# Two small products on a column of each value tile, ahead of the weighted sums of a local attention block

## The chip, the cores and the metric

The kernel runs on one core of one Trainium2 chip. The time is the device time in microseconds (us) of one execution; a kernel is run several times and the median is given. The profile is of one further execution, and its span runs from the first to the last instruction of the program.

## The reference

The input is 16 sequences of 256 rows with 128 features. After a layer norm, two branches are computed from it: a Mamba-like branch (projection, short convolution, a selective scan with 16 states) and a stack of six layers of local attention and feed-forward. The result is `x + s * silu(g)`. The part that matters here is the attention of the second branch, in float32:

```
q, k, v = split(x @ Wqkv)            # 16 heads of 64
q, k = normalized, scaled, rotated
windows of 32 queries; each sees its own 32 keys and the 32 before
sim  = q @ k.T * 8, masked
attn = softmax(sim)
out  = attn @ v                      # per head and window: 32x64 times 64x64
x    = out @ Wo + x
```

## The kernel before, in words

The attention is worked off in 192 blocks: six layers, 16 sequences, two blocks of 128 rows each. All of it is one program with an order written out by hand: the table `order` (lines 759 to 807) lists the steps of one turn of the main loop, and each step takes the block `n + ahead`. So one turn works on up to six blocks at different stages, and every engine executes its instructions in the order in which this table issues them. The semaphores between engines and DMA queues are put in by the framework from what each instruction reads and writes.

The steps around the change are these, for block `n`:

- `values` (472) multiplies the rows by the value weights (L427) into PSUM banks 4 and 5. `hand_out` (475) copies the result with ScalarE (L480) into the tile `vt`, in which every head has 64 value columns and a 65th that is one. Then SyncE issues DMAs that bring `vt` into `v2`: for each of two halves `r` (64 partitions, every second head) and each of four windows `j`, the 64 rows of keys that window `j` sees. An even block of a sequence takes 8 such DMAs (L492, L494), an odd one 10 (L491, L492, L494). `v2` exists once for even and once for odd blocks. `hand_out` of block `n + 1` stands just before `attend` of block `n`.
- `score` (575) lays the mask into PSUM (L587) and adds the products of queries and keys (L601): for eight column groups `c`, four windows `j` and two halves `r` one product with 64 rows and 32 columns of the array. A product in float32 is two weight loads and two matmuls in the records of the profile, so a block has 128 of each.
- `greatest` (L614) and `subtract` (L624) on VectorE, `soften` (L633) on ScalarE, then `turn_weights` (L552) transposes the weights and `turned_weights` copies them from PSUM into `aT` with ScalarE (L556).
- `attend` (644) makes the weighted sums (L657), again 64 products on tiles of 64 rows and 32 columns: tile (64 r, 32 j) of the array, weights `aT[rr, c, jj]`, moving `v2[rr, j, 65 columns of c]`. It takes `c = 7` first, into a bank of its own for each half (banks 7 and 6, `pav7`), then `c = 0` to `6` into banks 2 and 3 (`pav`), from which `subtract` of the following block has read the scores before. The 65th column of each sum is the softmax denominator.
- `divide_last` (665) takes the reciprocal of the denominators of `c = 7` on VectorE (L673) and scales on ScalarE (L674); `divide` (676) does the others on VectorE (L680, L681). `turn_out` transposes the result, `turned_out` copies it (L556), `close` (701) multiplies by `Wo` (L708).

Within one turn, TensorE's work ahead of `attend` is `project` of the keys of block `n + 4` and `values` of block `n + 1` (four L427 records each); the ScalarE step `square` (L438) of the queries, which reads banks 6 and 7, lies before it too. Behind it comes `turn` of the queries of block `n + 2` (L552). A scan step of the other branch and a part of a feed-forward (L326 to L375) are laid between these steps in every turn.

Of the kernel before, what the change touches and what calls it, by code (L numbers as in the profile page):

```python
# [18 lines left out]
H, DH, W = 16, 64, 32  # L19
# [11 lines left out]
def tile_kernel(ctx: ExitStack, tc: tile.TileContext, a, out):  # L31
    nc = tc.nc
# [14 lines left out]
    def pair(name):  # L47
        i = int(where[name])
        return psum[:, i : i + 2, :].rearrange("p b x -> p (b x)")

    def bank(name):
        return psum[:, int(where[name]), :]
# [591 lines left out]
    def attend(n):  # L644

        b = blocks[n]
        aT, v2 = b["aT"], v2s[b["blk"]]

        b["pav"] = pair("av").rearrange("p (r x) -> p r x", r=2)[:, :, 0 : 7 * VW]
        b["pav"] = b["pav"].rearrange("p r (c d) -> p r c d", c=7)  # L650
        b["pav7"] = [bank("e"), bank("l")]
        for c in (7, 0, 1, 2, 3, 4, 5, 6):
            for j in range(4):
                jj = slice(j * W, (j + 1) * W)
                for r in range(2):
                    rr = slice(r * 64, (r + 1) * 64)
                    nc.tensor.matmul(  # L657
                        b["pav7"][r][jj, 0:VW] if c == 7 else b["pav"][jj, r, c, :],
                        aT[rr, c, jj],
                        v2[rr, j, c * VW : (c + 1) * VW],  # L660
                        start=True,
                        stop=True,
                    )
# [87 lines left out]
    def feed():  # L751
# [35 lines left out]
        (rotate2, 4, 1),  # L787
        (add, 4, 1),
        (attend, 0),
        (divide_last, 0),  # L790
        (state, None, drive),
# [142 lines left out]
```

## Time and profile before

| | us |
|---|---|
| median of three runs | 3447.9 |
| lowest and highest | 3443.46, 3448.29 |
| the profiled execution, its own time | 3446.38 |
| its span | 3444.6 |

The granted TensorE clock of that execution has a mean of 0.988. The page of the profile gives the busy time of each engine (PE is TensorE's matmuls, PEld its weight loads, DVE is VectorE, ACT ScalarE, POOL GpSimd, SP SyncE, which only issues DMAs), the chain of work that ended last, and the costliest groups of instructions: line, engine, operation, the names of what is written and read, shapes, count, then busy time, the mean of one in ns, and the idle time of its engine just before it with what ended it. "issue" stands for waiting for nothing that the profile shows.

The rows of the steps around the change that are not taken up below:

```profile
L427 PE MATMUL psum<-wqkv,xT 128*128 128x512 f32 x2304 | 1070.3, 600 | 18.6 <-DVE cv L227 7.2
...
L438 ACT ACTIVATE sq<-psum 128x1024 f32<-128x1024 f32 x384 | 395.0, 1029 | 51.4 <-DVE t L459 51.0
...
L657 PEld LDWEIGHTS psum<-v,aT 64*32 64x32 f32 x24576 | 294.0, 105 | 200.9 <-issue 121.9
...
L480 ACT COPY vt<-psum 128x1024 f32<-128x1024 f32 x192 | 196.2, 1022 | 189.6 <-PE psum L427 189.6
...
v<-vt SPq DMA_DIRECT2D x1152, 130.0 KB, 2.4
```

The last of them is a row of the DMA issues: the transfers of L494, 1152 of them, of 130 KB each, take 2.4 us in the median from issue to landing. Busy time is a union, so records that overlap are counted once; the mean of one is its whole latency, which for a matmul on a small tile is much longer than the distance to the next one.

### The profile page before, as it was taken

The page shows a single profiled execution, that of the slowest core. Times are in us where ns is not written, and L with a number is a line of the kernel's source. Part 1 is how long each engine was busy: PE and PEld are TensorE (multiplying, and loading weights), DVE is VectorE, ACT ScalarE, POOL GpSimd, SP SyncE. Part 2 cuts the span into 40 slices and gives each one's busy share as a digit, 9 for nine tenths or more (in the row PEclk, how much of TensorE's full clock was granted, in tenths as well). Part 3 has the DMA queues.
Part 4 walks back from the last instruction along what each step waited for, and adds up shares of the span by engine and source line. Part 5 has one row for each costly group of instructions (what it writes and reads, how often), then busy time and mean ns, then how long its engine had stood idle before and what let it go on. Part 6 is the DMA issues. An engine that isn't in the chain of part 4 may idle for free.

```text
span 3444.6 us, 139812 instructions
## 1 busy us (share of the span) xinstructions
PE 3238.9 (94%) x62080; PEld 2163.4 (63%) x62080; DVE 2810.2 (82%) x3705; ACT 2123.3 (62%) x2725; POOL 2598.0 (75%) x2358
## 2 busy tenths in 40 slices
PE   6999999999999999999999999999999999999986
PEld 3666666666666666666666666666666666666663
DVE  6898879887898789878987889788879987777663
ACT  4666657655666566656665666576666665666554
POOL 6688868986898589968996789688878996565550
PEclk9999999999999999999999999999999999999998
DMA  3433334433333334333333333334333432222222
GB/s 87 104 98 105 84 84 104 104 81 83 97 97 90 91 94 97 91 85 88 107 92 91 88 96 92 89 99 98 91 81 93 105 94 70 69 64 70 63 64 57
DMA packets 190680, 304.49 MB, mean 88 GB/s; under 512 B 32702, under 2 KB 56572, under 8 KB 190076
## 3 DMA queue, kind: packets, MB, share of 16 engines
q1 hardware_dynamic: 189788, 295.22, 33.9%
q8 instruction: 488, 8.00, 1.0%
q14 instruction: 116, 0.95, 0.1%
q10 hardware_dynamic: 288, 0.33, 0.0%
HBM read 94.81 MB, written 8.91 MB: 30 GB/s over the span
## 4 chain that ended last, share of the span: by engine, by line
PE 73%; DVE 12%; ACT 6%; POOL 5%; issue 4%; DMA 0%; SPq 0%; DVEq 0%; ACTq 0%; POOLq 0%
PE psum L427 23%; PE psum L552 14%; PE psum L708 9%; PE psum L657 7%; PE psum L349 7%; PE psum L601 6%; PE psum L372 3%; ACT oT L556 3%; DVE t L459 2%; DVE o L681 2%; PE psum L587 2%; DVE hs L288 1%; DVE t L448 1%; POOL t L470 1%; DVE cv L227 1%
## 5 line engine op out<-in xcount | busy, mean ns | idle before, releaser
L470 POOL TENSOR_TENSOR t<-t,t 128x1024 f32<-128x1024 f32 x384 | 957.1, 2502 | 355.0 <-DVE t L459 184.4
L427 PE MATMUL psum<-wqkv,xT 128*128 128x512 f32 x2304 | 1070.3, 600 | 18.6 <-DVE cv L227 7.2
L542 POOL TENSOR_TENSOR t<-t,y 128x1024 f32<-128x1024 f32 x384 | 723.1, 1905 | 7.5
L427 PEld LDWEIGHTS psum<-wqkv,xT 128*128 128x128 f32 x2304 | 417.4, 192 | 406.0 <-issue 304.5
L448 DVE TENSOR_TENSOR t<-psum,tab 128x1024 f32<-128x1024 f32 x384 | 467.9, 1219 | 143.9 <-PE psum L427 131.1
L556 ACT COPY aT<-psum 128x1024 f32<-128x1024 f32 x192 | 194.2, 1012 | 589.6 <-PE psum L552 589.6
L459 DVE TENSOR_TENSOR t<-psum,tab 128x1024 f32<-128x1024 f32 x384 | 465.9, 1213 | 0.0
L504 DVE TENSOR_REDUCE ss<-sq 128x16 f32<-128x1024 f32 x384 | 456.4, 1198 | 1.3
L552 PE MATMUL psum<-ident,t 128*128 128x128 f32 x3072 | 412.7, 277 | 20.8 <-POOL t L542 8.9
L438 ACT ACTIVATE sq<-psum 128x1024 f32<-128x1024 f32 x384 | 395.0, 1029 | 51.4 <-DVE t L459 51.0
L657 PEld LDWEIGHTS psum<-v,aT 64*32 64x32 f32 x24576 | 294.0, 105 | 200.9 <-issue 121.9
L708 PE MATMUL psum<-oT,wo 128*128 128x256 f32 x1536 | 357.5, 386 | 24.2 <-ACT oT L556 24.2
L657 PE MATMUL psum<-v,aT 64*32 64x65 f32 x24576 | 332.8, 227 | 47.0 <-issue 24.6
L552 PEld LDWEIGHTS psum<-ident,t 128*128 128x128 f32 x3072 | 340.4, 142 | 40.3 <-POOL t L542 11.7
L708 PEld LDWEIGHTS psum<-oT,wo 128*128 128x128 f32 x1536 | 283.8, 190 | 81.4 <-ACT oT L556 46.5
L480 ACT COPY vt<-psum 128x1024 f32<-128x1024 f32 x192 | 196.2, 1022 | 189.6 <-PE psum L427 189.6
L601 PEld LDWEIGHTS psum<-kT,qT 64*32 64x32 f32 x24576 | 282.8, 105 | 11.2 <-issue 0.8
L601 PE MATMUL psum<-kT,qT 64*32 64x64 f32 x24576 | 286.2, 226 | 0.0
L288 DVE TENSOR_TENSOR_SCAN hs<-dA,bc 128x512 f32<-128x512 f32 x128 | 277.3, 2166 | 0.0
L556 ACT COPY oT<-psum 128x1024 f32<-128x1024 f32 x192 | 194.8, 1014 | 124.9 <-PE psum L552 123.0
L349 PE MATMUL psum<-xn,w 128*128 128x512 f32 (+1 forms) x576 | 260.2, 601 | 6.0 <-ACT o L674 4.8
L624 DVE TENSOR_TENSOR at<-psum,top 128x1024 f32<-128x1024 f32 x192 | 235.1, 1225 | 25.3
(102 smaller groups left out, 4583.0 us busy)
## 6 DMA issues: line engine op xcount, KB each, us to landing
v<-vt SPq DMA_DIRECT2D x1152, 130.0 KB, 2.4
bc<-rows SPq DMA_DIRECT2D x128, 512.0 KB, 5.1
v<-vt SPq DMA_DIRECT2D x576, 65.0 KB, 2.5
wqkv<-in_Wqkv SPq DMA_DIRECT2D x18, 512.0 KB, 4.0
wo<-in_Wo SPq DMA_DIRECT2D x6, 512.0 KB, 4.0
first<-in_x SPq DMA_DIRECT2D x8, 256.0 KB, 5.0
xn<-xT SPq DMA_DIRECT2D x16, 128.0 KB, 2.4
pad<-xn SPq DMA_DIRECT2D x8, 256.0 KB
```

The costliest lines, as they stand in the source:

```text
L349: nc.tensor.matmul(ph[0:n, i * G : (i + 1) * G], w1[:, i * DI + c0 : i * DI + c0 + n], xn, start=True, stop=True,)
L427: nc.tensor.matmul(pq[:, cc], xb, wq[:, cc], start=True, stop=True)
L448: nc.vector.tensor_tensor(t1.rearrange("p (h d) -> p h d", h=H), b["pq", i].rearrange("p (h d) -> p h d", h=H), table(n, i, 0).unsqueeze(1 ...
L459: nc.vector.tensor_tensor(t2.rearrange("p (h f d) -> p h f d", h=H, f=2), b["pq", i].rearrange("p (h f d) -> p h f d", h=H, f=2)[:, :, ::- ...
L470: nc.gpsimd.tensor_tensor(b["qk", i], b["qk", i], b["t2", i], ALU.add)
L504: nc.vector.tensor_reduce(b["ss"][:, j * H : (j + 1) * H], b["sq", i].rearrange("p (h d) -> p h d", h=H), AX.X, ALU.add,)
L542: nc.gpsimd.tensor_tensor(t3, t3, b["inv"][:, j * H : (j + 1) * H].unsqueeze(2).to_broadcast([128, H, DH]), ALU.mult,)
L552: nc.tensor.transpose(pt[:, cc], of[:, cc], ident)
L556: nc.scalar.copy(to, pt.rearrange("p (c t) -> p c t", c=NP))
L601: nc.tensor.matmul(sc4[jj, r, c, :], qT[rr, c, jj], kT[rr, c, k0 : k0 + 64], start=False, stop=True, skip_group_check=True,)
L657: nc.tensor.matmul(b["pav7"][r][jj, 0:VW] if c == 7 else b["pav"][jj, r, c, :], aT[rr, c, jj], v2[rr, j, c * VW : (c + 1) * VW], start=Tru ...
L708: nc.tensor.matmul(b["pw"][:, 0:L], wo[:, c, :], b["oT"][:, c, :], start=(c == 0), stop=(c == NP - 1), skip_group_check=True,)
```

## The change

Ahead of the 64 weighted sums of a block, two more products are issued, one for each half `r`. The weights are those of the sum for `c = 7`, window 0; the moving operand is column 0 of the four slices of `v2` of that half, 64 rows and 4 columns with a stride of one slice. They write the corner of 32 partitions and 4 columns of the two banks `pav7`, which the sums of `c = 7`, `j = 0` write afterwards with `start=True`. Nothing reads what they compute. The rest of the kernel is as before.

```diff
@@ -649,6 +649,12 @@
         b["pav"] = pair("av").rearrange("p (r x) -> p r x", r=2)[:, :, 0 : 7 * VW]
         b["pav"] = b["pav"].rearrange("p r (c d) -> p r c d", c=7)
         b["pav7"] = [bank("e"), bank("l")]
+
+        for r in range(2):
+            rr = slice(r * 64, (r + 1) * 64)
+            nc.tensor.matmul(
+                b["pav7"][r][0:W, 0:4], aT[rr, 7, 0:W], v2[rr, :, 0], start=True, stop=True
+            )
         for c in (7, 0, 1, 2, 3, 4, 5, 6):
             for j in range(4):
                 jj = slice(j * W, (j + 1) * W)
```

## The prediction

> **What bounds the kernel now.** First the page: its busy line, then the chain of work that ended last, then the rows of the two groups of small products.
>
> ```profile
> PE 3238.9 (94%) x62080; PEld 2163.4 (63%) x62080; DVE 2810.2 (82%) x3705; ACT 2123.3 (62%) x2725; POOL 2598.0 (75%) x2358
> ...
> PE 73%; DVE 12%; ACT 6%; POOL 5%; issue 4%; DMA 0%; SPq 0%; DVEq 0%; ACTq 0%; POOLq 0%
> PE psum L427 23%; PE psum L552 14%; PE psum L708 9%; PE psum L657 7%; PE psum L349 7%; PE psum L601 6%; PE psum L372 3%; ACT oT L556 3%; DVE t L459 2%; DVE o L681 2%; PE psum L587 2%; DVE hs L288 1%; DVE t L448 1%; POOL t L470 1%; DVE cv L227 1%
> ...
> L657 PE MATMUL psum<-v,aT 64*32 64x65 f32 x24576 | 332.8, 227 | 47.0 <-issue 24.6 <-DVE at L624 14.4 <-ACT sq L438 6.6
> ...
> L601 PE MATMUL psum<-kT,qT 64*32 64x64 f32 x24576 | 286.2, 226 | 0.0
> ```
>
> TensorE sets the end: 94% busy, 73% of the chain, and L657, the weighted sums that the change precedes, has 7% of it. A DMA is nowhere in the chain. The odd thing is in the last two rows. Both groups have 24576 records (two for each float32 product, 128 a block in 192 blocks) on the same 64*32 tiles; L657 streams 65 columns instead of 64 (1.6% more), yet is busy 332.8 against 286.2 us, 16% more: 46.6 us, or 243 ns a block. That is beside its idle time.
>
> Where do these 243 ns lie? I took one block from the timeline:
>
> ```profile
> 1013.55 0.19 PEld L427 LDWEIGHTS psum<-wqkv,xT 128*128 128x128 f32 x1 [0.24 <-ACT aT L556]
> ...
> 1015.79 1.70 PE L657 MATMUL psum<-v,aT 64*32 64x65 f32 x128
> ...
> 1017.60 0.25 DVE L680 RECIPROCAL den<-psum 128x14 f32<-128x14 f32 x1 [0.54 <-PE psum L657]
> ```
>
> and asked in 10 ns windows how many L657 matmuls are in flight (the x), then the same of this block's L601:
>
> ```profile
> 1016.00:1016.01 0.01, 0.01 (x28) 1.00 0.00 0
> 1016.10:1016.11 0.01, 0.01 (x23) 1.00 0.00 0
> 1016.25:1016.26 0.01, 0.01 (x6) 1.00 0.00 0
> 1016.40:1016.41 0.01, 0.01 (x11) 1.00 0.00 0
> 1016.55:1016.56 0.01, 0.01 (x16) 1.00 0.00 0
> 1016.70:1016.71 0.01, 0.01 (x27) 1.00 0.00 0
> ...
> 1010.20:1010.21 0.01, 0.01 (x19) 1.00 0.00 0
> 1010.30:1010.31 0.01, 0.01 (x21) 1.00 0.00 0
> 1010.45:1010.46 0.01, 0.01 (x27) 1.00 0.00 0
> ```
>
> The clock is full (1.00). The sums start well (x28), fall to 6 for a third of their time, and recover; the scores never fall below 19. The single records say the same: over all blocks (medians), matmul 32 starts 268 ns after the first, matmul 48 at 673 ns, matmul 127 at 1479 ns: 8.4 ns a record, then 405 ns for 16 records (25 ns each), then 10.2 ns. In the slow stretch two records start every 42.5 ns. The trace's semaphore record has what beats with it: TensorE's own semaphore is raised at 1016.104, .146, .189, .231, .274, .316, .359 and .401, eight times, 42.5 ns apart; matmuls start at 1016.142, .151, .193, .229, .236, .272, .278. Eight is the number of products for c = 7. In the program that this kernel builds to, each of these eight carries one wait (ScalarE, or one DMA semaphore) and each adds one to TensorE's semaphore; of the 56 behind them only the first waits (VectorE, L624), and only what others await adds, near the end (1 to 5 times). An addition stands on a product somebody awaits, or on one whose successor waits, because it can't be put off past a wait. Of the eight only the last two, j = 3, are awaited (L673). So the reading: the waits themselves cost nothing, since all are satisfied; **the additions that they force cost TensorE a slow stretch**.
>
> **The change, part by part.**
>
> *It removes* the waits of the eight products. Both small products read column 0 of all four v2 slices of their half and column group 7 of aT, thus everything the eight wait for. L657's own c = 0 to 6 show that a second reader of a slice gets no wait. What is left in this stretch: additions on the first small product (the second one waits) and on the two awaited ones: three instead of eight. Price of one: at the later pace of 10.2 ns the 16 slow records would take 163 ns instead of 405; 242 ns over eight is 30 ns. Five less: 151 ns a block. Bounds: the full spacing, 5 x 42.5 = 212 ns; from below nothing, if the stretch has another cause. The Trainium skill (TensorE: Matmul & The Clock Gate, "The cost: per-tile semaphore tail") says that increments of concurrent tiles serialize at some 26.3 ns each, and that one on the last is enough: 5 x 26.3 = 132 ns by the rule. The row decides: 151.
>
> *It adds* two products, in float32 four weight loads and four matmul records of 4 columns, on tiles (0,0) and (64,0). As stream: 4 x 10.2 = 41 ns. A rule speaks against this: TensorEngine Tiling, "Instruction Overhead", has a product with one column take as long as one with 60. By the rule the two tiles go through 18 full passes instead of 16; at 1479/16 = 92 ns a pass that is 185 ns, more than the saving. The trace sits between: eight records start in 56 ns in the queued part at the start, so a tile can turn a 65-column pass in 56 ns (two: 112 ns), while the later pace is 8 x 10.2 = 82 ns a pass; a tile that lags by 112 ns can catch up 26 ns a pass over 14 passes. I take the stream's 41 ns and keep 0 and 185 as ends. They write the corner [0:32, 0:4] of the banks that c = 7 then overwrites on the same engine; nobody reads it.
>
> *It moves* waits to the front: for an even block one ScalarE and eight DMA semaphores now stand before the first weighted sum, for an odd one ten DMAs. An instruction holds one wait, the others become semaphore instructions on TensorE's queue, 51 ns each by L657's rows: I count 4 (even) or 5 (odd) where there are 1 or 2 now, so 3 x 51 = 153 ns more. What hides it: in the timeline TensorE's sequencer is held by aT until 1013.47 and by the square (which ends 1014.40), and after that it runs ahead of the four L427 records until 1015.79, 1.4 us. Cover gone, it is 153 ns a block, 23 us in all. Queued behind are 128 sums, whose end L680 awaits. The DMAs: v2 of a block is issued one turn before its use (issues at 1000.00 to 1005.88 for the sums at 1015.79), landing takes 2.4 us in the median, 6.3 at most: long there, so demanding j = 3 first costs nothing. No DMA, no ScalarE, VectorE, POOL or SP instruction is added or moved.
>
> *The sum:* 151 - 41 = 110 ns a block. How much counts: L657's 7.4% of the chain (the chain's own answer) is 255 us, in pieces of 1.63 to 1.72 us, thus 153 of 192 blocks; and L680 waits for L657 153 times (113.0 us). 153 x 0.110 = 16.8 us. Before a matmul of L657 TensorE stood idle for "issue" 21 times, 24.6 us, each time with a 16 KB instruction transfer begun 2.2 to 2.9 us earlier; such a block (11%) gives its gain back to the fetch: 15 us. What is late next is the old chain, shifted: L680, L681, the turn of o. From the profiled span of 3444.6 us (3446.4 with what lies around it) this makes 3431; from the median of 3447.9, which I use, **3433 us**.
>
> The instruction stream is an unknown of its own. Each block gets 8 records and about 3 semaphore instructions more, so the places where fetches fall shift against the blocks. "issue" idles on TensorE come to some 40 us in all; their positions drift through the blocks and come back about every 430 us. With another drift I expect the same sum, give or take 10 us.
>
> **Rivals.**
> 1. *As forecast*, chance 0.62: 3433, between 3424 (212 - 30 ns) and 3441.
> 2. *The products take back the gain*, 0.19: the two first tiles lag by two full passes and the rest waits for them. 151 - 185 = -34 ns, or at 56 ns a pass +39: between +5 and -6 us, so 3448 or thereabouts. For it: the rule, and the 82 ns a pass. Against: the slack of 26 ns a pass.
> 3. *Slower: the additions aren't the cause*, 0.13. Then the stretch is TensorE's queue run dry (it begins after 33 loads and 33 matmuls, where what was queued during L427 would end), it stays, and the change is pure added work: 41 to 185 ns x 153 blocks, +6 to +28 us: 3465 in the middle. It decides if less than 41 of the 242 ns are the additions'. Against it: the 42.5 ns beat, and that L601, queued as long behind L587, has no such stretch.
> 4. *The change doesn't do what it says*, 0.06: the waits stay on the eight, for instance as a semaphore is awaited anew for each slice; 153 x 41 ns is 6 us, 3454. Against: c = 0 to 6.
>
> **How the numbers follow.** What this measurement can tell from no change is about 0.2%, 7 us (the three runs spread by 4.9). Faster: most of the first case and a bit of the second with luck in the fetches, 0.67. Same: the rest of the first, most of the second, half of the fourth, 0.20. Slower: the third and the other half, 0.13. The range reaches from 3405, the full 212 ns with every block on the chain, no cost of the products (-36 us) and good fetches, to 3451, where the second case ends; the third's middle lies outside. The first case's own range is 3424 to 3441.
>
> **What would show it.** In the changed profile L657 (both small products get a line of their own) should be busy some 1.6 us a block instead of 1.73, about 310 us in all; the windows should have no stretch of 6 in flight, but two or three short dips; semaphore instructions of TensorE rise to about 860 on the new line; L680's wait shrinks by about 0.1 us a time. If L657 keeps 330 us, the third case holds; if the dip is gone but the end of the sums isn't earlier, the second. A DMA named as the releaser of the small products would make the whole argument wrong.

## The result, and the profile after

The changed kernel takes 3460.51 us in the median of 16 runs (3448.23 to 3470.26), the kernel before 3447.03 in 16 runs on the same chips (3437.98 to 3453.92). The ratio is 1.0040, with a 95% interval of 1.0029 to 1.0052: slower by 0.4%, where 0.4% faster was forecast, and outside the range. The profiled execution has a span of 3461.4 us.

The page after, in the same parts as before: busy time by engine, the chain that ended last, and the row of the weighted sums, which are now on L663.

```profile
PE 3241.1 (94%) x62848; PEld 2157.8 (62%) x62848; DVE 2807.5 (81%) x3705; ACT 2118.5 (61%) x2725; POOL 2593.1 (75%) x2358
...
PE 71%; DVE 12%; POOL 6%; ACT 5%; issue 4%; DMA 0%; SPq 0%; DVEq 0%; POOLq 0%; ACTq 0%
...
L663 PE MATMUL psum<-v,aT 64*32 64x65 f32 x24576 | 317.5, 226 | 57.1 <-issue 45.2
```

The sums have become shorter, 317.5 us of busy time after 332.8 (about 310 was forecast). But the idle time before them that ended for no visible reason ("issue") has grown from 24.6 to 45.2 us; in a second profile of each kernel it is 27.6 and 36.6 us. VectorE's reciprocal (L680, now L686), which waits for the last sums, stood waiting for 119.7 us in all where it was 113.0; forecast was 0.1 us less each time. The two small products are a line of their own; this is what the view of one source line says of it (count, then shortest, median and longest duration in ns):

```profile
L655 PEldq EVENT_SEMAPHORE  x863: 51/51/51, 71.2 to 3408.6; - x173
...
L655 PE MATMUL psum<-v,aT x768: 164/169/213, 73.4 to 3408.8; 64*32 64x4 f32 x192
```

So 863 semaphore instructions stand where 286 did, as counted in the prediction (some 860). Next, the matmuls of L663 in flight in 10 ns windows, in the block whose windows were shown of before; the offsets from its first sum are about the same.

```profile
1022.06:1022.07 0.01, 0.01 (x23) 1.00 0.00 0
1022.21:1022.22 0.01, 0.01 (x13) 1.00 0.00 0
1022.36:1022.37 0.01, 0.01 (x19) 1.00 0.00 0
```

The stretch with 6 in flight is gone; what is left is a short dip to 13. By the single records (medians over the blocks), the last sum starts 1362 ns after the first instead of 1479, and the first one 549 ns after the last value product instead of 523. From that product to the last sum it is 1911 ns where it was 2002: **the change saves 91 ns a block, and the kernel is still slower.**

Where the time went can be seen in one block. TensorE's timeline of the changed kernel, and after it that of the kernel before in a block that lies in about the same place of the instruction stream:

```profile
1506.83 1.53 PE L663 MATMUL psum<-v,aT 64*32 64x65 f32 x121
1509.38 0.27 PE L663 MATMUL psum<-v,aT 64*32 64x65 f32 x2 [1.02 <-issue]
```

```profile
2161.84 1.70 PE L657 MATMUL psum<-v,aT 64*32 64x65 f32 x128
```

In the changed kernel TensorE stops for 1.02 us in front of the last two records of the sums, with no semaphore to wait for. The trace of DMA packets tells what it waits for. TensorE's instructions come in transfers of 16384 bytes, 256 instructions each (488 of them for the 124,979 instructions of the kernel before). These are the packets around the two blocks, of the changed kernel from 1506.7 to 1506.8 us (a digit is 2.5 ns), and of the kernel before from 2160.8 to 2161.0 us (5 ns):

```profile
DMA  0000000000000000000000090000000000000000
q8 instruction: 1, 0.02, 82.1%
```

```profile
DMA  0000000090000000000000000000000000000000
q8 instruction: 1, 0.02, 30.1%
```

In the changed kernel the transfer begins at 1506.76, 0.04 us *before* the first sum (1506.80), and the sums go on 2.62 us after that; in every such stall of the two profiles it is 2.2 to 3.0 us. In the block of the kernel before, the transfer begins at 2160.84, 1.00 us before the first sum (2161.84), and nothing stops. A block of the changed kernel consumes its 256 instructions of sums in 1.4 us. So the start of the transfer decides, and the change moved it by about one microsecond.

That these gaps are waits for instructions can be seen by counting: over the 17 kept traces TensorE has 661 gaps for "issue", and behind all but 2 of them the next instruction has the same place in the stream, number 193 or 194 of a group of 256.

### The profile page after: what moved, and what is told of

Read it like the earlier page. It is cut to its first block, busy times and chain, and to the rows that moved or that the text cites. A ratio compares the mean times of both kernels' runs of the same rounds, so it can differ in the third digit from the quotient of the medians.

```text
span 3461.4 us, 141925 instructions
## 1 busy us (share of the span) xinstructions
PE 3241.1 (94%) x62848; PEld 2157.8 (62%) x62848; DVE 2807.5 (81%) x3705; ACT 2118.5 (61%) x2725; POOL 2593.1 (75%) x2358
## 4 chain that ended last, share of the span: by engine, by line
PE 71%; DVE 12%; POOL 6%; ACT 5%; issue 4%; DMA 0%; SPq 0%; DVEq 0%; POOLq 0%; ACTq 0%
PE psum L427 22%; PE psum L552 13%; PE psum L714 9%; PE psum L349 7%; PE psum L663 7%; PE psum L601 6%; PE psum L372 3%; ACT oT L556 3%; DVE t L459 2%; POOL t L542 2%; DVE hs L288 2%; DVE o L687 2%; POOL t L470 1%; PE psum L587 1%; DVE t L448 1%
## 5 line engine op out<-in xcount | busy, mean ns | idle before, releaser
L438 ACT ACTIVATE sq<-psum 128x1024 f32<-128x1024 f32 x384 | 395.0, 1029 | 51.2 <-DVE t L459 51.2
L714 PE MATMUL psum<-oT,wo 128*128 128x256 f32 x1536 | 357.5, 386 | 24.4 <-ACT oT L556 24.4
L663 PE MATMUL psum<-v,aT 64*32 64x65 f32 x24576 | 317.5, 226 | 57.1 <-issue 45.2
L663 PEld LDWEIGHTS psum<-v,aT 64*32 64x32 f32 x24576 | 275.1, 105 | 67.8 <-issue 52.4
```

The lines of the kernel that those rows point to most:

```text
L663: nc.tensor.matmul(b["pav7"][r][jj, 0:VW] if c == 7 else b["pav"][jj, r, c, :], aT[rr, c, jj], v2[rr, j, c * VW : (c + 1) * VW], start=Tru ...
L714: nc.tensor.matmul(b["pw"][:, 0:L], wo[:, c, :], b["oT"][:, c, :], start=(c == 0), stop=(c == NP - 1), skip_group_check=True,)
```

## The experiments

The quantities below come from each kernel's trace. *Issue idle*: gaps over 150 ns between TensorE's matmuls that ended for "issue"; *short* are those under 1.5 us each, *long* the others. *Transfer start*: the median start of an instruction transfer against the first sum, for even and odd blocks of a sequence; negative is earlier. It is taken in the blocks where the end of a transfer's 256 instructions falls into about the last 50 of the sums, so that it can stall them, from transfers begun in the 2 us around the first sum (from 1.7 before to 0.3 after). A median is over 3 to 19 transfers, single ones lie more than 1 us off it, and other limits move some medians by 0.1 to 0.2 us. A figure after a stroke is a second profile.

| kernel | ratio to before | issue idle, us | of it short, us | transfer start even, odd (us) | first to last sum, ns |
|---|---|---|---|---|---|
| before | 1 | 38.2 / 45.0 | 22.1 / 21.6 | -1.14, -0.22 | 1479 |
| the change | 1.0040 | 60.2 / 50.2 | 41.2 / 33.7 | -0.05, -0.07 | 1362 |
| odd blocks alone | 1.0056 | 50.3 / 49.0 | 22.0 / 26.6 | -1.14, -0.11 | both kinds |
| even blocks alone | 1.0042 | 53.0 | 29.4 | -0.07, -0.24 | both kinds |
| products behind c = 7 | 1.0050 | 53.3 / 42.0 | 23.6 / 20.1 | -1.19, -0.21 | 1513 |
| one such product | 1.0040 | 43.4 | 24.4 | -1.17, -0.13 | 1495 |
| one product over 128 rows | 0.9976 | 24.0 | 10.8 | -0.95, -0.82 | 1324 |
| a transfer cut in two | 1.0034 | 45.2 / 51.3 | 28.4 / 28.5 | -0.25, -0.14 | 1481 |
| stream shifted by 128 | 0.9993 | 36.1 | 15.9 | -1.16, -0.42 | 1479 |
| bf16 product ahead | 0.9917 | 15.8 | 8.8 | -1.42, -0.82 | 1324 |
| the same and the change | 0.9951 | 16.2 | 10.6 | -1.25, -1.13 | 1362 |
| bf16 and products behind c = 7 | 0.9945 | 18.8 | 10.1 | -1.26, -0.58 | 1358 |

The second profiles of the first two rows missed what was expected of them. The kernel before was to show 38 us of issue idle again, within 5, and showed 45.0; the change was to show 60 us within 8, of them 41 us within 5 in short ones, and showed 50.2 and 33.7. So such a sum moves by 7 to 10 us from one execution to the next. The places are steadier: of the 21 blocks of the kernel before whose sums stalled for issue, 17 stalled in both profiles, and of 39 of the change, 30.

The row of before holds the first lead: its odd blocks are as late as the change's. In the program, an odd block has one more DMA behind the window 0 of each half than an even one, so that its *second* sum needs two waits; in this program a weight load holds one of them, and a semaphore instruction with the other stands between the first and the second sum. Even blocks have none there. The change puts two between its two small products in every block. **Theory A:** such an instruction behind the first product of the block keeps TensorE's sequencer from running ahead, and with it the request for the next instructions. **Theory B:** it is the number of added instructions, or the faster sums, that brings more blocks into stalls.

### One half of the change at a time

```diff
-        for r in range(2):
+        for r in range(2 if b["blk"] == 1 else 0):
```

> The two small products in odd blocks alone. A stall is the time by which the start of the last weighted sum of a block lies later than usual, without those in which VectorE is awaited at record 16: 31.0 us in 27 blocks before, 58.5 us in 44 blocks after. Theory A (a semaphore instruction between the first two products of a block keeps TensorE's sequencer from running ahead, so that the next 16 KB of instructions are asked for too late): odd blocks had one there already, so the stalls stay near 31 us, and 96 blocks gain 117 ns in the sums and lose 79 ns to the products: ratio 0.998 to 1.001. Theory B (it is the number of added instructions, or the faster sums, that brings more blocks to the end of what was fetched): half of the change, half of the added stalls, 45 us, ratio about 1.002.

Ratio 1.0056 (1.0042 to 1.0070). The short idle times stayed at those of before (22.0 us) and even blocks kept their early transfer, as theory A has it. The time did not: it is a miss for both, by 16 us for the upper end of A's range and by 12 us for B. The long idle times grew, to 28.3 us in 10 (16.1 in 7 before, 23.4 in 11 in its second profile).

```diff
-        for r in range(2):
+        for r in range(2 if b["blk"] == 0 else 0):
```

> The two small products in even blocks alone. Theory A: even blocks had no semaphore instruction between their first products and now get some, so all of the added stalls come from here: about 58 us in some 44 blocks, ratio 1.004 to 1.006. Theory B: half of the change, 45 us, ratio about 1.002.

Ratio 1.0042 (1.0025 to 1.0058), within A's range. Now the even blocks' transfers start at -0.07 us, and the stalls in the sums of even blocks are 23.7 us (6.0 before, about 10 in its second profile); odd blocks have fewer, 17.6. In all 41.4 us, less than A's 58.

### The same instructions without moving a wait

```diff
         for c in (7, 0, 1, 2, 3, 4, 5, 6):
+            for r in range(2 if c == 0 else 0):
+                rr = slice(r * 64, (r + 1) * 64)
+                nc.tensor.matmul(
+                    b["pav"][0:W, r, 0, 0:4], aT[rr, 7, 0:W], v2[rr, :, 0], start=True, stop=True
+                )
```

> The same two products in each block, but between the sums of c = 7 and those of c = 0, into the bank corner of c = 0: no wait of c = 7 is moved, no semaphore instruction and no addition to TensorE's semaphore is added or taken away, only 8 instructions a block. Theory A: the stalls stay near 31 us; the time of a block's sums is 1479 ns plus 40 to 80 ns: ratio 1.001 to 1.003. Theory B: the stalls grow as in the full change, to 50 us or more, and no gain stands against them: ratio 1.006 or more.

> As the two products between c = 7 and c = 0, but one alone: 4 instructions a block. Theory B, as luck of where the boundaries meet the big loads of the scan: the work itself costs 15 to 20 ns a block (3 us), the rest is chance, anything from 0.998 to 1.005, and its idle times for issue differ from both neighbours. If each added instruction costs by itself: half of the two products' loss, 1.0025.

Two products: 1.0050 (1.0036 to 1.0064); one: 1.0040 (1.0028 to 1.0052). They cost 34 and 16 ns a block in the records, 6.5 and 3 us in all, and leave the short idle times where they were. The rest of the loss, some 10 us, neither theory had. The second profile of the first,

> The two products between c = 7 and c = 0 on the kernel before, for a second profile: if its loss lies in the idle times of 1.5 us and more (29.7 us in 13 in the first, 16 to 23 in the kernel before), they are above 25 us again; if that was chance, 16 to 23.

had long idle times of 21.9 us instead of 29.7, so these vary from one execution to the next. And of the odd blocks alone,

> The change in odd blocks alone, for a second profile: idle times of 1.5 us and more above 25 us again (28.3 in the first), those below 1.5 us again 22 us as in the kernel before; if the first was chance, the long ones are at 16 to 23 us.

the second profile had 22.4 us in long and 26.6 in short ones: here too the long ones are not above 25 again.

### All waits ahead of a single product

```diff
-        for r in range(2):
-            rr = slice(r * 64, (r + 1) * 64)
-            nc.tensor.matmul(
-                b["pav7"][r][0:W, 0:4], aT[rr, 7, 0:W], v2[rr, :, 0], start=True, stop=True
-            )
+        nc.tensor.matmul(
+            b["pav7"][0][0:W, 0:4], aT[:, 7, 0:W], v2[:, :, 0], start=True, stop=True
+        )
```

> One small product over all 128 rows instead of two over 64: all waits of c = 7 and all semaphore instructions stand ahead of it, none between the first products of a block; additions to TensorE's semaphore among the first eight sums fall from eight to two. Theory A: the stalls go from odd blocks too, below 10 us in all; the sums stay at about 1362 ns; the array changes from 128 to 64 rows in between, some 0 to 100 ns: ratio 0.990 to 0.997. Theory B: 5 to 6 more instructions a block and the same fast sums, stalls of 50 us, ratio 1.000 to 1.004.

Ratio 0.9976 (0.9965 to 0.9987), just outside what A gave. Most transfers are early, in odd blocks too, and the short idle times halve; but 24.0 us of issue idle remain, where A had below 10. The sums are faster here than in the change, so it is not their speed that brings the stalls. Its local account is nil: the sums take 1324 ns, 155 less than before, but the product and the change from 128 to 64 rows cost 155 ns ahead of them (678 instead of 523 ns from the last value product). What it gains, it gains in idle time.

### A semaphore instruction alone

```diff
-            nc.sync.dma_start(out=v2[o + W : o + 64, 0, :], in_=vt[0:W, r, :])
+            for i in range(2 if r and not blk else 1):
+                at = slice(i * 16, i * 16 + 16) if r and not blk else slice(0, W)
+                nc.sync.dma_start(out=v2[o + W :, 0, :][at], in_=vt[at, r, :])
```

> The kernel before, with one transfer of the even blocks (second half, window 0) cut in two of 16 rows each. On TensorE this puts one semaphore instruction between the first two weighted sums of each even block, as odd blocks have it already, and nothing else: no product, no addition. Theory A (that semaphore instruction holds back the sequencer and with it the next instruction transfer): even blocks in which a 16 KB boundary of the instruction stream lies 5 to 28 products into the sums stall by about 1.2 us each as odd ones do, 15 to 20 us more in the sums of even blocks, ratio 1.004 to 1.006. Theory B (places of the 16 KB boundaries, shifted by added instructions): one instruction in two blocks shifts hardly anything, ratio 0.999 to 1.002.

This adds to TensorE's program nothing but one semaphore instruction between the first two sums of each even block. The transfer start of even blocks moves from -1.14 to -0.25 us: this part of A is shown by the one thing changed. The ratio, 1.0034 (1.0023 to 1.0044), is close to A's and outside B's; by itself it decides little, since kernels that don't touch this wait lose as much (the two products behind c = 7). The stalls are smaller than A had, 28.4 us of short idle time after 22, where 15 to 20 us more were expected: where the late transfer occurs in an even block, the sums stop for 0.5 to 1.05 us; and in some of the exposed even blocks the transfer had come earlier (two of 11 by more than 1 us), for a reason that I don't know.

> The kernel with the cut transfer once more for a second profile: its profile was of an execution 10 us faster than its median. Idle times below 1.5 us again 28 us within 4; the longer ones, 16.8 us before, higher.

The second profile agrees in the short ones (28.5 us) and has 22.8 us in long ones.

### Is it the place in the stream?

```diff
+        for _ in range(32):
+            nc.tensor.matmul(
+                bank("n")[0:W, 0:4], ident[0:64, 0:W], ident[0:64, 0:4], start=True, stop=True
+            )
         norms = [first_norm(0), first_norm(1)]
```

> The kernel before with 32 small products (128 instructions) at the very start, while TensorE has nothing to do yet: every place of the instruction stream moves by half of a 16 KB part against the blocks, and nothing else changes. If the place of the boundaries alone decides and the kernel before has a lucky one (theory D, which would explain the losses of the kernels that only add instructions), ratio 1.002 to 1.006 and more long idle times; if the places even out over 192 blocks, 0.999 to 1.001.

Ratio 0.9993 (0.9985 to 1.0001): moving all boundaries by half of a part changes nothing in the time that can be told, though the short idle times are 15.9 us instead of 22. Against this shift at least, the kernel before does not live on a lucky place.

### The waits taken elsewhere

```diff
     def values(n):
+        if n:
+            v2 = v2s[blocks[n - 1]["blk"]]
+            nc.tensor.matmul(
+                pair("v")[:, 0:4], ident_h, v2[:, :, 0:1].bitcast(BF)[:, :, 1], start=True, stop=True
+            )
         blocks[n]["pv"] = product(n, 2, pair("v"))
```

> One product in bf16 on all 128 rows and columns, with the identity as weights and one bf16 half of column 0 of the v2 tile, ahead of the value product, into a corner of the bank which that product overwrites. It takes the DMA waits of the sums 2 us before them, in the array mode of its neighbours; the sums keep one wait (ScalarE) and two additions, no semaphore instruction. Theory A: no block has such an instruction within the sums, so the stalls in the sums nearly go (below 10 us); the sums fall to 1330 ns as in the single product, without its change of mode; the product costs 60 to 200 ns ahead of the value product: ratio 0.986 to 0.994. If stalls only move to the place of the semaphore instructions or come by chance: 0.994 to 1.000.

Ratio 0.9917 (0.9902 to 0.9931): 3425.1 us, faster than both kernels. The waits for the DMAs are taken four matmuls earlier, on all 128 rows and columns like the products around it. Issue idle falls to 15.8 us.

To this kernel the two small products of the change are added:

```diff
     def attend(n):
...
+        for r in range(2):
+            rr = slice(r * 64, (r + 1) * 64)
+            nc.tensor.matmul(
+                b["pav7"][r][0:W, 0:4], aT[rr, 7, 0:W], v2[rr, :, 0], start=True, stop=True
+            )
```

> The bf16 product ahead of the value product, and the change's two small products as well: TensorE executes all that the change executes and 2 instructions more, but no semaphore instruction stands between the first products of a block. Theory A: the next instruction transfer starts some 0.8 us earlier than in the change, the idle time for issue stays below 25 us (60.2 in the change, 15.8 with the bf16 product alone), the time is that of the bf16 product alone plus about 27 to 80 ns a block, ratio 0.992 to 0.997. Theory B (added instructions): idle time for issue of 45 us or more, ratio 0.999 to 1.004.

Ratio 0.9951 (0.9939 to 0.9964). This is the run that decides most between A and B. TensorE does all the work of the change here, in the same order, with more instructions; but the products find their DMA waits done, so no semaphore instruction stands among them. The transfers start at -1.25 and -1.13 us, and the rows of who waited (times, total, longest) read, for the change and for this kernel:

```profile
PE psum L663 <- issue: 45.2, 39, 3.3
```

```profile
PE psum L668 <- issue: 7.8, 10, 2.2
```

39 stalls become 10, and the kernel is 0.9% faster than the change though its sums take the same 1362 ns. Against the bf16 product alone the small ones cost 65 ns a block (27 ahead, 38 within the sums), and the ratio rises by 0.0034, 11.7 us; 192 x 65 ns are 12.5 us. Without stalls, the added work costs what its records say.

> The bf16 product ahead of the value product, with the two small products between c = 7 and c = 0. If the loss of these two (ratio 1.005 on the kernel before, of which their own work is 0.0015) comes from late instruction transfers that the waits among the sums cause, it is not there now: 0.9917 plus 0.001 to 0.002, thus 0.992 to 0.995, idle time for issue below 22 us. If added instructions cost by themselves: 0.996 to 0.998 and 25 us or more.

Ratio 0.9945 (0.9933 to 0.9957), idle 18.8 us: the two products behind c = 7 cost 0.0028 here, 10 us, against 0.0050 on the kernel before.

## Why the prediction was wrong

Point by point:

- *What bounds the kernel, and the slow stretch*: right. The beat of 42.5 ns came from the additions, and it went with them. I counted five fewer; the program has six fewer, since the first small product adds nothing either: in the trace only two records at the head of a block raise TensorE's semaphore. With six gone and no small products among the sums (one product over 128 rows), the sums take 1324 ns: 155 ns less, 26 ns an addition. I forecast 151 in all; that it came so close is luck, since my price of 30 ns a piece was too high and the count too low. The 26.3 ns of the Trainium skill (TensorE: Matmul & The Clock Gate, "The cost: per-tile semaphore tail") were the better price.
- *The products at 41 ns*: 27 ns ahead of the sums and 38 within them, 65 in all (1911 less 523 less 1324 gives 64). A size too small, between the stream's 41 and the tile's 185. The saving is then 91 ns a block and not 110, some 14 us for the 153 blocks on the chain.
- *The waits moved to the front, "153 ns, hidden"*: **this is the step that failed.** I gave 153 ns of semaphore instructions a cover of 1.4 us in which TensorE's sequencer runs ahead, and priced only their own length. The length was hidden in most blocks: the first sum starts 549 ns after the last value product, 26 more than before. It shows in some 12 blocks in which TensorE waits for the ScalarE square (L438) in front of the sums: there the sums start 0.2 us later than before, under 3 us in all. What the sequencer does meanwhile I had put at nothing. With semaphore instructions between the two small products, the next instruction transfer starts in even blocks 0.05 us before the first sum instead of 1.14, and a block with a boundary in the wrong place then mostly stops for 0.7 to 1.3 us. Issue idle rose by 13.6 us (means of two profiles), as much as the sums gained. I had asked only who waits for the instruction's end, not what the sequencer would have begun meanwhile.
- *The instruction stream, "the same sum, give or take 10 us"*: wrong in kind. I treated it as chance of position. Position has a part (16 us of short idle time in the shifted stream after 22), but the sum depends more on what stands among the first products: 20 to 27 us of short idle time where odd blocks alone have semaphore instructions there, unshifted; 28 to 29 where even ones get them too at the old pace or without the odd ones' products; 34 to 41 in the change; 9 to 11 where none has them. The evidence was in the first trace: before L657 odd blocks stood idle for issue for 19.7 us and even ones for 4.9, and I looked only at the total.
- *Two slips*: by the cases as I gave them, slower is 0.13 + 0.03, not 0.13; and 16 records in 405 ns are two in 51 ns in the median, while 42.5 ns is the beat of the one block shown.

The account of the change in us: 14 gained in the sums, under 3 lost in the twelve blocks; issue idle from 41.6 to 55.2 (means of two profiles), 13.6 lost; and the clock. Over the runs on record the granted clock has a mean of 0.9839 in 16 of the change and of 0.9859 in 31 of the kernel before; 0.002 of the time is 7 us, and among those 31 an execution whose clock is lower by 0.001 is 3 us longer in the mean. That is some 9 us slower in all, where 13.5 were measured; the rest is not accounted for, and sums of issue idle move by more than that from one execution to the next.

Why the clock is lower is not shown. In the profiles 96 us of the execution are at half clock before and 116 after (means of two). Half of these 20 us lie between 60 and 2900 us, where 8 of the change's 11 stretches of half clock (3.4 or 6.8 us each) begin within 1.5 us of the end of a stall of 1.9 us or more; the other half lie at the start and in the last layer, where both kernels wait for other engines. No run took the clock's part away alone.

Of the rivals, none was this. The third (additions not the cause) and the second (products take back all) are excluded by the sums' 1362 ns; the fourth by the program. The sign of the third came true by luck, for a reason that I had named only as noise.

**What stays open.** Kernels that add two or four matmul records to the block behind c = 7, or the change in odd blocks alone, lose 0.4 to 0.6% with short idle times about as before. Their own work explains 3 to 6.5 us of it, or a gain; the long idle times, most of them behind the scan's 512 KB loads, were more in the first profiles and less in the second ones. A lower granted clock (means of 0.9848 and 0.9845 for two products and one, 0.9830 for odd blocks alone, after 0.9855 to 0.9859 in the kernel before beside them) is worth some 2, 5 and 9 us. So a cost of whatever is added to the block, beside late transfers, is not excluded. With the waits taken elsewhere, the products behind c = 7 cost 10 us, the half of it. What the other half is, the runs don't show. Nor do they show why a semaphore instruction delays the transfer, only that it does. It isn't that the instruction itself is executed late: in odd blocks of the kernel before, the one between the first two sums starts 1.28 us before the first sum (median), and the transfer only 0.2 us before it. That the sequencer is held back meanwhile is theory A's reading of this.

## What to carry to other kernels

Before a burst of many small matmuls, see that all waits are taken ahead of its first product, not between the first and the second: here the next instruction transfer then started about a microsecond earlier. A cheap product that touches the awaited tile, put ahead of products on the same rows and columns of the array, does it (here -0.8%, with fewer additions to the engine's semaphore as well). When a trace has stalls "for issue" in some blocks only, sort them by what differs between these blocks before calling them chance.

## What the hardware showed that I had not expected

- TensorE's instructions come in transfers of 16384 bytes, and a stall ends 2.2 to 3.0 us after the start of one. A burst on eight tiles uses 256 instructions in 1.4 us, so a transfer that starts with the burst was late by 1.0 us in the block shown. The Trainium skill (Runtime: NRT & Kernel Launch, "Instruction fetch mechanics") holds this refill to be mostly hidden, as the sequencer needs some 20 cycles for an instruction; here 256 loads and matmuls start within 1.36 us, 5 ns each, and the idle time was 38 to 60 us of an execution of the two kernels. The measurement decides.
- One semaphore instruction between the first two products of a burst moved the transfer by 0.9 us (-1.14 to -0.25 us, the transfer cut in two).
- Before each of the 8 long idle times of the change's first profile (1.6 to 3.3 us, 19.1 us in all), a 512 KB load of the scan (L270) had been issued 3.7 to 5.6 us before the instruction transfer began, with half clock for 3.4 us or more near several of them. That the load makes the transfer late was not tried.
